# Two sums of a second attention moved into the last iterations of a graph attention, and a conditioning product cut into quarters

## The chip, the cores and the metric

The kernel runs on one core of a Trainium2 chip. The metric is the device time of one execution in microseconds, the median of the runs made of one kernel. One execution was also taken by the hardware profiler; all durations in this document come from such an execution.

## The reference

Two blocks follow each other on x of 4 batches x 1024 rows x 512 columns, all in float32.

- A graph attention. Each row goes through a linear layer (with a conditioning vector beside it), and then attends, with 16 heads and in two directions, to the first 20 rows of its batch; a mask of 11 labels gives each pair a bias and can switch it off. The result goes through relu and is added to x.
- A transformer block with adaptive normalization. The conditioning vector c (one row of 512 per batch) gives six rows of 512 by one product, the *modulation*:

```python
mod = silu(c) @ W_mod + b_mod                       # 512 -> 6 x 512
sh_msa, sc_msa, g_msa, sh_mlp, sc_mlp, g_mlp = split(mod, 6)
x = x + g_msa * attention(layernorm(x) * (1 + sc_msa) + sh_msa)   # 16 heads of 64, W_qkv, W_out, b_out
x = x + g_mlp * ff(layernorm(x) * (1 + sc_mlp) + sh_mlp)          # 512 -> 2048 -> 512, gelu
```

## The kernel before

Every instruction is issued in the order in which the program writes it: each engine (TensorE, VectorE, ScalarE, GpSimd, and SyncE, which starts the transfers) works off its own queue in that order, and waits between the engines come from the tiles that they share. A tile has a tag, and tiles of one tag take turns in as many buffers as the tag has; a new tile may be written only when the last reader of the tile before it in that buffer is done.

**Graph attention** (from about 60 to 418 us) is a loop `for s in range(-4, NTA + 2)` over 32 blocks of 128 rows. It is software-pipelined: iteration s works on several blocks at once, each in another step. In the order of one iteration, what matters here is:

- `g_load`, `g_loadmask`, `g_modload`: transfers that SyncE starts (block s + 4; weights of the modulation).
- `g_scores(s)` (TensorE, L710, 16 matmul passes into `pa`), then `g_weightsT(s - 1)` (TensorE, L759, five transposes of the finished weights `wts`, copied by ScalarE at L760).
- `g_soft1` to `g_soft5` (the softmax of block s): VectorE L723 (mask factor), GpSimd L733 (mask bias added), VectorE L740 and L741 (maximum, subtraction), ScalarE L744 (exp), VectorE L749 and L750 (sum, reciprocal), GpSimd L752 (`wts`). Between them `g_mask1(s + 3)` on GpSimd (L690, L692) and `g_mask2(s + 2)` on VectorE (L699 to L703).
- `g_self(s + 2)` (TensorE, L670), `g_selfT(s + 1)` (TensorE, L683, into a PSUM tile of tag `tr`, which has one buffer), `g_attend(s - 1)` (TensorE, L774).
- `g_rows(s - 1)` (VectorE, L786, and the store of the finished rows `x1d`, L787), `g_start(s + 3)` (VectorE, L658 and L659), `g_sum(s + 4)` (ScalarE, L646: the sum of each row of x, with the copy itself thrown into a tile `junk`).
- At the end of some iterations a round of the modulation, `g_mod(r)`. It multiplies half of the columns of several of the six rows: 16 matmuls of 256 columns into `pm` (tag `tr`, L811), four column groups of 32 beside each other. A round of kind 0 (shift and scale rows; r = 0 and 1, in iterations 6 and 12) is copied to `mrow` by ScalarE (L828), transposed by TensorE (L831, tag `tr`) and taken by VectorE into `modT` (L835, L839). A round of kind 1 (gate rows; r = 2 and 3, in iterations 22 and 29) is taken by VectorE straight from `pm` into `gates` (L820, L823). Their weights `wm` are loaded by `g_modload` in iterations 1, 7, 13 and 23.
- Rows of the second block's first batch that are already finished are normalized here: `norm_row` (VectorE, L389; iterations 15, 16, 22, 23) and `norm_T` (iterations 17 to 20 and 24 to 27): four transposes on TensorE into `ptn` (tag `tr`, L407), taken by ScalarE into `hT` (L412). The first query and key product (`ahead`, L442) follows in the last iterations.

**The second attention** uses a scheme of seven block products for every eight (`seven`, `with_two`), and so needs sums of blocks of the rows (`row_sums`: four subtractions of 128x1024, over `hT`, into `tx` and one in place) and of the weights (`weight_sums`: four of 128x256, into `ex` and one in place). For the first values of the first batch these sums stand between the two stages. VectorE forms the row sums (L579, L580, L584, L586) and GpSimd the weight sums (L468 to L471):

```python
first_sums, more_sums = row_sums(0)
first_sums()
for k in range(2):
    more_sums(k, nc.vector)
emit(-3, 0)                          # weight_sums on GpSimd, among others
for s in range(NS + 1):
    ...                              # scores, maximum, exp, scaling, transposes of step s
```

Each step s of that loop computes scores (TensorE, L1079, `psc`), their maximum (VectorE, L1090), exp (ScalarE, L1096), the division by the sum (ScalarE L1103, GpSimd L1105) and transposes (VectorE, L1114, with SyncE's transfers, L1118). A planner puts the products of the next queries, keys and values (TensorE, L497, with copies by ScalarE, L508, L519, and additions by VectorE, L511), the weighted values (L1041) and the output projections (L1059) between the scores.

Of the kernel before, what the change touches and what calls it, by code (L numbers as in the profile page):

```python
# [12 lines left out]
F32 = mybir.dt.float32  # L13
I32 = mybir.dt.int32
AF = mybir.ActivationFunctionType
ALU = mybir.AluOpType
# [3 lines left out]
P = 128  # L20
S = 1024
F = 512
# [19 lines left out]
def cond_block_kernel(  # L42
# [32 lines left out]
    def row(ap):  # L75

        return ap.unsqueeze(0)
# [54 lines left out]
    with ExitStack() as gctx:  # L132
# [9 lines left out]
        scT = gp.tile([P, FC, 32], F32, name="scT")  # L142
        wb = gp.tile([P, NL], F32, name="wb")
        bb = gp.tile([P, 1], F32, name="bb")
        bmB = gp.tile([P, F], F32, name="bmB")
        boB = gp.tile([P, F], F32, name="boB")


        lp = gctx.enter_context(tc.tile_pool(name="lp", bufs=1, reuse_waits="tile"))
# [219 lines left out]

        rp = ctx.enter_context(tc.tile_pool(name="rp", bufs=1, side="right", reuse_waits="tile"))  # L370
        qp = ctx.enter_context(tc.tile_pool(name="qp", bufs=1, side="right", reuse_waits="tile"))
        VB = 4
        xl, hT, wqk, wv, qT, kT, w1g, part = {}, {}, {}, {}, {}, {}, {}, {}
        NORM = ((x1d, mv1, rs1, nm1, SH_A, SC_A), (x2d, mv2, rs2, nm2, SH_M, SC_M))
# [189 lines left out]
        def of_weights(key, w, which, c):  # L564
# [3 lines left out]
            h, f = PIECE[which]  # L568
            return w[:, 2 * f + c, h, :]

        def row_sums(b):

            tx[b] = xp.tile([P, 6, F], F32, name="tx", tag="tx")
            h0, h1 = hT[0, 2 * b], hT[0, 2 * b + 1]
            o = [tx[b][:, 2 * k : 2 * k + 2, :] for k in range(3)]
            b11, b12, b21, b22 = h0[:, :2, :], h1[:, :2, :], h0[:, 2:, :], h1[:, 2:, :]

            def one():
                nc.vector.tensor_tensor(o[0], b12, b11, ALU.subtract)  # L579
                nc.vector.tensor_tensor(o[1], b22, o[0], ALU.subtract)  # L580

            def two(k, e=nc.gpsimd):
                if k == 0:
                    e.tensor_tensor(b12, b22, b12, ALU.subtract)  # L584
                else:
                    e.tensor_tensor(o[2], b21, o[1], ALU.subtract)  # L586

            return one, two
# [53 lines left out]
        def g_sum(i):  # L642

            nzs[i] = wp.tile([P, 1], F32, name="nz", tag="nz", bufs=4)
            junk = wp.tile([P, F], F32, name="junk", tag="junk", bufs=1)
            nc.scalar.activation(junk, xs[i], AF.Copy, accum_out=nzs[i])  # L646

        def opened(t):

# [139 lines left out]

        mods = {}  # L790

        CW = F // 2

        def g_modload(r):
            kind, half = divmod(r, 2)
            if r == 2:
                for k, (at, bias) in enumerate(((2 * F, b_out), (5 * F, b2))):
                    nc.sync.dma_start(bmB[64 * k : 64 * (k + 1)], row(b_mod[at : at + F]).broadcast_to([64, F]))
                    nc.sync.dma_start(boB[64 * k + 32 : 64 * k + 64], row(bias).broadcast_to([32, F]))
            mods[r] = wp.tile([P, FC, 4, CW], F32, name="wm", tag="wm", bufs=1)  # L800
            for k, blk in enumerate(((0, 1, 3, 4), (2, 5))[kind]):
                at = blk * F + half * CW
                nc.sync.dma_start(mods[r][:, :, k, :], w_mod[:, at : at + CW].rearrange("(c p) f -> p c f", p=P))

        def g_mod(r):

            kind, half = divmod(r, 2)
            pm = ps.tile([P, F], F32, name="pm", tag="tr")
            for c in range(FC):
                for k in range(4):  # L810
                    nc.tensor.matmul(  # L811
                        pm[32 * k : 32 * (k + 1), :CW],
                        lhsT=scT[:, c, :],
                        rhs=mods[r][:, c, k if kind == 0 else k // 2, :],
                        start=(c == 0),
                        stop=(c == FC - 1),
                    )
            cols = slice(half * CW, (half + 1) * CW)
            if kind == 1:
                nc.vector.tensor_tensor(gates[:, cols], pm[:, :CW], bmB[:, cols], ALU.add)  # L820
                for k in (1, 3):
                    q = slice(32 * k, 32 * (k + 1))
                    nc.vector.tensor_tensor(gates[q, cols], gates[q, cols], boB[q, cols], ALU.mult)  # L823
                if half == 1:
                    nc.sync.dma_start(gated, gates)
                return
            mrow = wp.tile([P, F], F32, name="mrow", tag="junk", bufs=1)
            nc.scalar.copy(mrow[:, :CW], pm[:, :CW])  # L828
            pt = ps.tile([P, 2, 4, 32], F32, name="ptm", tag="tr")
            for c in range(2):  # L830
                nc.tensor.transpose(pt[:, c].rearrange("p k b -> p (k b)"), mrow[:, c * P : (c + 1) * P], ident)  # L831
            for k, blk in enumerate((0, 1, 3, 4)):
                v = V_MOD + blk * FC + 2 * half
                o = modT[:, k * FC + 2 * half : k * FC + 2 * half + 2, :]
                nc.vector.tensor_tensor(  # L835
                    o, pt[:, :, k, :B], vecs[:, v : v + 2].unsqueeze(2).to_broadcast([P, 2, B]), ALU.add
                )
                if k % 2 == 1:
                    nc.vector.tensor_scalar(o, o, 1.0, None, ALU.add)  # L839

# [17 lines left out]
        for s in range(-4, NTA + 2):  # L858
            do(g_load, s + 4)
            if s >= -2:  # L860
                do(g_loadmask, s + 4)
            if s in (1, 7, 13, 23):
                g_modload(s // 6)
            do(g_scores, s)
            if s == NTA:
                ahead(4)
            do(g_weightsT, s - 1)
            do(g_soft1, s)
            do(g_startscores, s + 1)
            do(g_startattend, s - 1)  # L870
            do(g_soft2, s)
            do(g_mask2, s + 2)
            do(g_mask1, s + 3)
            do(g_soft3, s)
            do(g_self, s + 2)
            if s >= NTA - 2:
                ahead((2, 1, 1, 0)[s - NTA + 2])
            do(g_selfT, s + 1)
            do(g_soft4, s)
            if 0 <= s - 2 < NTA:  # L880
                statistics(xs.pop(s - 2), mv1[:, s - 2, :], wp)
            do(g_soft5, s)
            do(g_attend, s - 1)
            do(g_selfout, s + 2)
            do(g_rows, s - 1)
            do(g_start, s + 3)
            do(g_sum, s + 4)

            if s in (6, 12, 22, 29):
                g_mod((s - 5) // 6 - s // 29)  # L890
            if s == 12:
                rstd(rs1, mv1, nm1, 0, NT)
            if s in (14, 21):
                norm_load(0, s // 7 - 2)
            if 15 <= s - s // 22 * 7 <= 16:
                for i in range(2):
                    norm_row(0, s // 22 * VB + 2 * ((s - 15) % 7) + i)
            if s in (17, 18, 19, 20, 24, 25, 26, 27):
                norm_T(0, s // 24, (s - 17) % 7, bank_l0)
            if s == 25:  # L900
                load_qk(0, 0)
                load_v(0, 0)
                load_qk(0, 1)
# [3 lines left out]

    xp = ctx.enter_context(tc.tile_pool(name="xp", bufs=1, side="right", reuse_waits="tile"))  # L910
    vp = ctx.enter_context(tc.tile_pool(name="vp", bufs=1, side="right", reuse_waits="tile"))
    octx = ctx.enter_context(ExitStack())
    op_ = octx.enter_context(tc.tile_pool(name="op", bufs=1, side="right", reuse_waits="tile"))
# [2 lines left out]
    with ExitStack() as actx:  # L916
# [55 lines left out]

        def short():
            return op_.tile([P, F], F32, name="s", tag="s", bufs=1)

        def home_ex():
            return xp.tile([P, 3 * HB], F32, name="ex", tag="ex", bufs=1)

        def qk_sums(b, gp):
            weight_sums(nc.gpsimd, ("qk", b, gp), wqk[b, gp], home_ex)  # L980
# [182 lines left out]
        for b in range(B):  # L1163
            s0 = b * NP * NT
            for kind, n, lo, hi in ORDER:
                if b == 0 and lo < 8:
                    if (kind, n) == ("qk", 0):
                        ends[kind] = ends[kind][1:]
                        continue
                    lo, hi = (0, 0) if kind == "v" else (4, 4)  # L1170
                units, load, sums, steps = (
                    (1, load_qk, qk_sums, qk_steps) if kind == "qk" else (1.05, load_v, v_sums, v_steps)
                )
                if b > 0 or lo >= 8:
                    old = ends[kind].pop(0)
                    if old is not None:
                        behind.append((len(fill), old, 1))
                    add(-1, -1, 0, 0, load, b, n)
                if chain:
                    behind.append((len(fill), chain[-2], 0))  # L1180
                add(-1, -1, 0, 4, sums, b, n)
                add_steps(s0 + lo, s0 + hi, units, steps(b, n))
                ends[kind].append(chain[-1])
            for gp in range(NP):
# [166 lines left out]
                for _, k in sorted((f[3], k) for k, f in enumerate(fill) if where[k] == s):  # L1351
                    fill[k][4]()

        first_sums, more_sums = row_sums(0)
        first_sums()
        for k in range(2):
            more_sums(k, nc.vector)
        emit(-3, 0)
        before = None
        for s in range(NS + 1):  # L1360
# [224 lines left out]
```

## Time and profile before

| | |
|---|---|
| median of 3 runs | 3083.87 us (3083.62 to 3086.13) |
| the profiled execution | 3087.44 us, its span 3085.6 us |
| granted TensorE clock, mean | 0.998 |
| TensorE matmuls, busy | 3036.6 us, 98% of the span |
| VectorE, ScalarE, GpSimd, busy | 64%, 46%, 38% |
| TensorE's waits from 60 to 418 us, largest | 4.6 us for `wts` (L752), 2.2 us for `mrow` (L828) |
| TensorE's waits from 418 to 520 us, largest | 2.3 us for `w` (L1096), 1.9 us for `q` (L511) |

In a row of the timeline the first number is the start in microseconds from the start of the span, the second the duration from the first start to the last end of the merged instructions; then the engine (PE = TensorE, PEld = its weight loads, DVE = VectorE, ACT = ScalarE, POOL = GpSimd, SP = SyncE), the line of the kernel, the operation, output<-inputs, sizes, and how many instructions the row stands for. Square brackets give the idle time of the engine just before, and what ended it.

### The profile page before, as it was taken

What the parts mean: (1) busy time and instruction counts of PE and PEld (TensorE: products, weight loads), DVE (VectorE), ACT (ScalarE), POOL (GpSimd) and SP (SyncE); (2) the same over time, 40 slices, a digit from 0 to 9 for tenths busy, and PEclk for the clock granted to TensorE, in tenths of its full rate; (3) what the DMA queues carried; (4) which work ended last, traced back from release to release, by engine and by line L of the source; (5) the groups of instructions that cost most, each with busy time, mean ns of one, the idle gap of its engine ahead of it and who ended that gap; (6) DMA issues with size and microseconds to landing.
All of it is one profiled execution on the core that took longest, in us unless ns stands there. A gap on an engine that the chain in (4) does not pass through costs nothing.

```text
span 3085.6 us, 40768 instructions
## 1 busy us (share of the span) xinstructions
PE 3036.6 (98%) x14977; PEld 1918.0 (62%) x14977; DVE 1982.7 (64%) x2772; ACT 1420.5 (46%) x2351; POOL 1187.9 (38%) x729
## 2 busy tenths in 40 slices
PE   9999999999999999999999999999999999999999
PEld 5666655455455455455455455455568888888888
DVE  3788867777878777778777778777764332223222
ACT  2444456555655555655555655555641221112211
POOL 1444446455455554455545454654531101111010
PEclk9999999999999999999999999999999999999999
DMA  6433438677778766777776777776772011101110
GB/s 193 127 128 110 130 98 202 154 167 165 187 176 202 176 160 165 190 175 192 179 169 157 185 183 179 184 174 150 191 184 87 27 35 41 48 14 42 35 41 14
DMA packets 281882, 418.00 MB, mean 135 GB/s; under 512 B 28272, under 2 KB 100012, under 8 KB 281684
## 3 DMA queue, kind: packets, MB, share of 16 engines
q1 hardware_dynamic: 281436, 415.05, 53.1%
q8 instruction: 120, 1.97, 0.3%
q14 instruction: 78, 0.64, 0.1%
q10 hardware_dynamic: 248, 0.34, 0.0%
HBM read 121.09 MB, written 25.76 MB: 48 GB/s over the span
## 4 chain that ended last, share of the span: by engine, by line
PE 75%; DVE 7%; DMA 4%; ACT 4%; SPq 3%; issue 3%; POOL 3%; POOLq 0%; ACTq 0%; DVEq 0%
PE q L497 16%; PE psc L1079 13%; PE pav L1041 13%; PE pout L1059 7%; PE mbd L497 5%; PE mbu L497 5%; PE mad L497 3%; PE mau L497 3%; SPq L1118 2%; ACT w L1096 2%; PE mcd L497 2%; PE mdd L497 2%; DMA wT<-wd 2%; PE mdu L497 2%; PE mcu L497 2%
## 5 line engine op out<-in xcount | busy, mean ns | idle before, releaser
L1105 POOL TENSOR_SCALAR w<-w,sm 128x1024 f32<-128x1024 f32 x256 | 733.3, 2864 | 887.9 <-DVE sm L1101 876.2
L1096 ACT ACTIVATE w<-psc,mx 128x1024 f32<-128x1024 f32 x512 | 570.6, 1114 | 650.8 <-DVE mx L1090 649.7
L1114 DVE STREAM_TRANSPOSE wd<-w 128x1024 f32<-128x1024 f32 x512 | 633.6, 1238 | 132.7 <-ACT w L1103 115.9
L1090 DVE TENSOR_REDUCE mx<-psc 128x1 f32<-128x1024 f32 x512 | 599.4, 1211 | 100.8 <-PE psc L1079 97.9
L1079 PE MATMUL psc<-kT,qT 64*128 64x512 f32 x2048 | 530.0, 615 | 7.9 <-ACT w L1096 5.3
L1041 PE MATMUL pav<-wT,v 128*64 128x256 f32 x4096 | 476.4, 382 | 2.6 <-DMA wT<-wd 2.4
L1041 PEld LDWEIGHTS pav<-wT,v 128*64 128x64 f32 x4096 | 291.0, 137 | 226.0 <-issue 65.8
L1079 PEld LDWEIGHTS psc<-kT,qT 64*128 64x128 f32 x2048 | 203.3, 186 | 261.8 <-issue 154.9
L1103 ACT ACTIVATE w<-w,sm 128x1024 f32<-128x1024 f32 x256 | 291.0, 1137 | 0.0
L1059 PE MATMUL pout<-wout,oT 128*128 128x512 f32 x512 | 241.7, 605 | 0.0
L476 POOL TENSOR_TENSOR tx<-hT 128x512 f32<-128x512 f32 x8 | 10.2, 1269 | 601.4 <-DVE hT L414 601.4
L497 PE MATMUL q<-hT,wqk 128*128 128x512 f32 (+1 forms) x396 | 185.6, 593 | 7.3 <-DVE q L511 7.3
L1059 PEld LDWEIGHTS pout<-wout,oT 128*128 128x128 f32 x512 | 92.2, 189 | 129.3 <-issue 116.3
L710 PE MATMUL pa<-kp,sfT 128*128 128x320 f32 x512 | 143.5, 433 | 1.4 <-ACT sfT L685 1.4
L519 ACT COPY mbu<-mau 128x512 f32<-128x512 f32 x30 | 17.1, 570 | 276.4 <-PE mau L497 269.8
L1067 DVE TENSOR_TENSOR xr<-pout,xr 128x512 f32<-128x512 f32 x128 | 85.5, 680 | 90.1 <-PE pout L1059 90.0
L497 PEld LDWEIGHTS q<-hT,wqk 128*128 128x128 f32 x396 | 73.6, 191 | 103.8 <-issue 100.2
L497 PE MATMUL q<-tx,ex 128*128 128x512 f32 (+1 forms) x264 | 126.5, 603 | 0.0
L710 PEld LDWEIGHTS pa<-kp,sfT 128*128 128x128 f32 x512 | 94.8, 190 | 38.2 <-ACT sfT L685 1.9
L670 PE MATMUL pf<-wx,xT 128*128 128x512 f32 x256 | 116.3, 597 | 0.9 <-DVE pf L659 0.9
L497 PE MATMUL mad<-w,hs 128*128 128x256 f32 x512 | 113.1, 379 | 0.0
L497 PEld LDWEIGHTS mad<-w,hs 128*128 128x128 f32 x512 | 97.3, 190 | 13.2
(285 smaller groups left out, 4214.1 us busy)
## 6 DMA issues: line engine op xcount, KB each, us to landing
wT<-wd SPq DMA_DIRECT2D x1024, 256.0 KB
wqk<-in_w_qkv SPq DMA_DIRECT2D x64, 256.0 KB
xT<-in_xt SPq DMA_DIRECT2D x32, 256.0 KB
xs<-in_x SPq DMA_DIRECT2D x32, 256.0 KB
x1d<-xs SPq DMA_DIRECT2D x32, 256.0 KB
xl<-x1d SPq DMA_DIRECT2D x32, 256.0 KB
wv<-in_w_qkv SPq DMA_DIRECT2D x32, 256.0 KB
xr<-x1d SPq DMA_DIRECT2D x32, 256.0 KB
```

What stands on the lines that cost most here:

```text
L497: nc.tensor.matmul(t[:, q * width : (q + 1) * width], lhsT=lhs(which, q, k), rhs=rhs(which, q, k), start=(fresh and q == 0 and k == 0), st ...
L670: nc.tensor.matmul(pfs[i], lhsT=xT[i][:, c, :], rhs=wx[:, c, :], start=False, stop=(c == FC - 1), skip_group_check=True,)
L710: nc.tensor.matmul(pas[i][:, n, :HF], lhsT=sfT2[i][:, c, :], rhs=kp[:, b, c, n * HF : (n + 1) * HF], start=False, stop=(c == FC - 1), skip ...
L1041: nc.tensor.matmul(po[j * D : (j + 1) * D, :], lhsT=vt[b, g][:, m, p * P + j * D : p * P + (j + 1) * D], rhs=w[:, j, :, m, :], start=(m == 0),
L1059: nc.tensor.matmul(po, lhsT=oT[b, 2 * g + p][:, n * P : (n + 1) * P], rhs=wout[b, g][:, p, :], start=(p == 0), stop=(p == 1),)
L1067: nc.vector.tensor_tensor(t, po, t, ALU.add)
L1079: nc.tensor.matmul(sc[j][:, n * F : (n + 1) * F], lhsT=qT[b, gp][q, t * P : (t + 1) * P], rhs=kT[b, gp][q, n * F : (n + 1) * F], start=Tru ...
L1090: nc.vector.tensor_reduce(mx, sc, axis=AX.X, op=ALU.max, negate=True)
L1096: nc.scalar.activation(w, sc, AF.Exp, bias=mx, accum_out=sm)
L1103: nc.scalar.mul(w, w, sm)
L1105: nc.gpsimd.tensor_scalar(w, w, sm, None, ALU.mult)
L1114: nc.vector.transpose(wd[j][:, :, at, :], wn.pop((b, gp, t, j)).rearrange("p (m k) -> p m k", k=U))
```

## The change

- The row sums for the first values are formed in the graph attention's last iterations: two of them in iteration 28 and one in iteration 29, on GpSimd; the fourth, which overwrites a part of `hT` that TensorE still reads there, stays behind the loop, and is on GpSimd too. The weight sums are formed in iteration 30, on GpSimd as before. For this the pool that holds `tx` and `ex` is opened before the loop.
- To make room in SBUF, the modulation goes in eight rounds of a quarter of the columns (128) in place of four of a half: kind 0 in iterations 3, 6, 9, 12, kind 1 in iterations 15, 18, 21, 24, each with its weights loaded two iterations earlier and, for kind 1, the bias rows in quarters too. The sum of each row of x writes its copy over x itself, and the tile `junk` is gone.

```diff
-        bmB = gp.tile([P, F], F32, name="bmB")
-        boB = gp.tile([P, F], F32, name="boB")
+        bmB = gp.tile([P, F // 4], F32, name="bmB")
+        boB = gp.tile([P, F // 4], F32, name="boB")
...
+        xp = ctx.enter_context(tc.tile_pool(name="xp", bufs=1, side="right", reuse_waits="tile"))
...
-            def one():
-                nc.vector.tensor_tensor(o[0], b12, b11, ALU.subtract)
-                nc.vector.tensor_tensor(o[1], b22, o[0], ALU.subtract)
+            def one(e=nc.vector):
+                e.tensor_tensor(o[0], b12, b11, ALU.subtract)
+                e.tensor_tensor(o[1], b22, o[0], ALU.subtract)
...
-            junk = wp.tile([P, F], F32, name="junk", tag="junk", bufs=1)
-            nc.scalar.activation(junk, xs[i], AF.Copy, accum_out=nzs[i])
+            nc.scalar.activation(xs[i], xs[i], AF.Copy, accum_out=nzs[i])
...
-        CW = F // 2
+        CW = F // 4
...
-            kind, half = divmod(r, 2)
-            if r == 2:
+            kind, part_ = divmod(r, 4)
+            cols = slice(part_ * CW, (part_ + 1) * CW)
+            if kind == 1:
                 for k, (at, bias) in enumerate(((2 * F, b_out), (5 * F, b2))):
-                    nc.sync.dma_start(bmB[64 * k : 64 * (k + 1)], row(b_mod[at : at + F]).broadcast_to([64, F]))
-                    nc.sync.dma_start(boB[64 * k + 32 : 64 * k + 64], row(bias).broadcast_to([32, F]))
+                    at += part_ * CW
+                    nc.sync.dma_start(bmB[64 * k : 64 * (k + 1)], row(b_mod[at : at + CW]).broadcast_to([64, CW]))
+                    nc.sync.dma_start(
+                        boB[64 * k + 32 : 64 * k + 64], row(bias[cols]).broadcast_to([32, CW])
+                    )
...
-                nc.vector.tensor_tensor(gates[:, cols], pm[:, :CW], bmB[:, cols], ALU.add)
+                nc.vector.tensor_tensor(gates[:, cols], pm[:, :CW], bmB, ALU.add)
...
-            mrow = wp.tile([P, F], F32, name="mrow", tag="junk", bufs=1)
-            nc.scalar.copy(mrow[:, :CW], pm[:, :CW])
-            pt = ps.tile([P, 2, 4, 32], F32, name="ptm", tag="tr")
-            for c in range(2):
-                nc.tensor.transpose(pt[:, c].rearrange("p k b -> p (k b)"), mrow[:, c * P : (c + 1) * P], ident)
+            mrow = wp.tile([P, CW], F32, name="mrow", tag="mrow", bufs=1)
+            nc.scalar.copy(mrow, pm[:, :CW])
+            pt = ps.tile([P, 4, 32], F32, name="ptm", tag="tr")
+            nc.tensor.transpose(pt.rearrange("p k b -> p (k b)"), mrow, ident)
             for k, blk in enumerate((0, 1, 3, 4)):
-                v = V_MOD + blk * FC + 2 * half
-                o = modT[:, k * FC + 2 * half : k * FC + 2 * half + 2, :]
-                nc.vector.tensor_tensor(
-                    o, pt[:, :, k, :B], vecs[:, v : v + 2].unsqueeze(2).to_broadcast([P, 2, B]), ALU.add
-                )
+                v = V_MOD + blk * FC + part_
+                o = modT[:, k * FC + part_, :]
+                nc.vector.tensor_scalar(o, pt[:, k, :B], vecs[:, v : v + 1], None, ALU.add)
...
-            if s in (1, 7, 13, 23):
-                g_modload(s // 6)
+            if 1 <= s <= 22 and s % 3 == 1:
+                g_modload(s // 3)
...
-            if s in (6, 12, 22, 29):
-                g_mod((s - 5) // 6 - s // 29)
+            if 3 <= s <= 24 and s % 3 == 0:
+                g_mod(s // 3 - 1)
...
+            if s == 28:
+                first_sums, more_sums = row_sums(0)
+                first_sums(nc.gpsimd)
+            if s == 29:
+                more_sums(1)
+            if s == 30:
+                weight_sums(nc.gpsimd, ("v", 0, 0), wv[0, 0], home_ex)
...
-                add(-1, -1, 0, 4, sums, b, n)
+                if (kind, b, n) != ("v", 0, 0):
+                    add(-1, -1, 0, 4, sums, b, n)
...
-        first_sums, more_sums = row_sums(0)
-        first_sums()
-        for k in range(2):
-            more_sums(k, nc.vector)
+        more_sums(0)
         emit(-3, 0)
```

## The prediction

> **What bounds the kernel now.** I read the page's busy row first, then the list of what TensorE waits for, by stretch, and then the timeline of graph attention (60 to 418 us) and of the change to the second attention.
>
> ```profile
> PE 3036.6 (98%) x14977; PEld 1918.0 (62%) x14977; DVE 1982.7 (64%) x2772; ACT 1420.5 (46%) x2351; POOL 1187.9 (38%) x729
> ```
>
> TensorE has work for 98% of the span, so only its 49 us of idle time can be won, while anything put in its way is paid at once: it takes its instructions in order. Next the timeline of TensorE. Below, T(s) is the first L759 of graph attention's iteration s, and offsets such as +5.7 count from it.
>
> ```profile
> 127.99 0.75 PE L759 MATMUL pt<-ident,wts 128*128 128x128 f32 x5
> 137.93 0.76 PE L759 MATMUL pt<-ident,wts 128*128 128x128 f32 x5
> 143.66 1.93 PE L811 MATMUL pm<-wm,scT 128*32 128x256 f32 x32
> 146.68 0.44 PE L831 MATMUL ptm<-ident,mrow 128*128 128x128 f32 x2 [1.08 <-ACT mrow L828]
> 151.26 0.71 PE L759 MATMUL pt<-ident,wts 128*128 128x128 f32 x5
> 266.85 0.77 PE L759 MATMUL pt<-ident,wts 128*128 128x128 f32 x5 [0.30 <-POOL wts L752]
> 272.50 0.60 PE L407 MATMUL ptn<-ident,xl 128*128 128x128 f32 x4
> 277.25 0.71 PE L759 MATMUL pt<-ident,wts 128*128 128x128 f32 x5
> 307.65 0.74 PE L759 MATMUL pt<-ident,wts 128*128 128x128 f32 x5
> 313.37 1.93 PE L811 MATMUL pm<-wm,scT 128*32 128x256 f32 x32
> 319.64 0.71 PE L759 MATMUL pt<-ident,wts 128*128 128x128 f32 x5
> ```
>
> A plain iteration (127.99 to 137.93) lasts 9.94. One with a shift-and-scale round, s = 6, lasts 13.33: the round sits at +5.7 and TensorE stands until ScalarE has copied `mrow`. With a gate round, s = 22, it is 11.99; with norm_T's four transposes, s = 18, 10.40 (they stand at +5.65). Now VectorE:
>
> ```profile
> 275.94 1.36 DVE L659 SCALAR_TENSOR_TENSOR pf<-qrB,nz,bsB 128x512 f32<-128x512 f32 x1
> 318.00 0.41 DVE L820 TENSOR_TENSOR gates<-pm,bmB 128x256 f32<-128x256 f32 x1
> 339.78 1.36 DVE L659 SCALAR_TENSOR_TENSOR pf<-qrB,nz,bsB 128x512 f32<-128x512 f32 x1
> ```
>
> VectorE's queue ends an iteration with L659, and the gate round's L820 comes after that: at s = 22 TensorE ended `pm` at 315.2, and VectorE read it only at 318.00, +10.35. VectorE's own cycle is 9.95 (L723 to L723), just over TensorE's 9.85, so it has no room to come earlier. Last the place that is to become shorter, all engines:
>
> ```profile
> 418.82 1.22 DVE L579 TENSOR_TENSOR tx<-hT 128x1024 f32<-128x1024 f32 x1
> 420.19 2.02 PE L497 MATMUL q<-ex,tx 128*128 128x128 f32 x16 [0.22 <-DVE tx L579]
> 422.36 1.22 DVE L586 TENSOR_TENSOR tx<-hT,tx 128x1024 f32<-128x1024 f32 x1
> 423.49 2.35 DVE L1090 TENSOR_REDUCE mx<-psc 128x1 f32<-128x1024 f32 x2
> 426.00 3.11 PE L1079 MATMUL psc<-kT,qT 64*128 64x512 f32 x8 [2.00 <-ACT w L1096]
> 429.29 2.02 PE L497 MATMUL q<-ex,tx 128*128 128x128 f32 x16 [0.18 <-issue]
> ```
>
> Four row sums hold VectorE from 418.82 to 423.57, and the first maximum waits behind them although its scores were done at 420.0.
>
> **What the change takes away at that place.** The maximum then starts 2.0 after the scores (417.98), as at 476.41 to 478.43 where nothing is ahead of it: 420.0 for 423.49, 3.49 earlier. The second scores can start when the first value products end (423.8) and end at 425.8 for 429.1. The next products wait for ScalarE's copy L519 (ended 429.19), which moves with the maximum. So TensorE gains 3.3 to 3.5. I take 3.5. Its ends are 4.75 (all four sums) and 0 (see the rivals). The waits after that hang on VectorE and ScalarE, so they move along. `more_sums(0)` moves to GpSimd: a 128x1024 subtraction is about 2.4 there (256 columns take 0.72 and 512 take 1.27 to 1.28, so 2.1 ns each more); between TensorE's last read of hT at 416 and GpSimd's first own work (L1105, 427.37 now, 423.9 then) it has room; its reader is the third value step (435.9). The weight sums (4 x 0.72) ran on GpSimd at 411.2 to 414.1, under work: moving them wins nothing.
>
> **What the quarters cost: shift and scale, four rounds for two (s = 3, 6, 9, 12).** Now s = 6 takes 13.33 and s = 7 and 8 give back 0.13, since VectorE's cycle gets slack: 3.26 a round. The copy starts at +8.32 because ScalarE's queue holds exp, the `sf` copy and the sum of x before it, not because of `pm`: shorter matmuls win nothing. Won is 0.1 of the copy (0.37 for 256 columns) and one transpose of 0.13: 3.03 a round. Two more rounds, and two that are 0.23 shorter: 6.06 - 0.46 = 5.6. The six small VectorE operations a round (0.15 to 0.17) lie after L659, where such an iteration has over 2 us free.
>
> **Gates, four rounds for two (s = 15, 18, 21, 24 for 22, 29).** `pm` with 128 columns: no row shows it; half of 1.93 is 0.97, its 32 weight loads took 1.45; I take 1.0, and it matters only at s = 21. VectorE's three gate operations are 0.41 to 0.42 each at 256 columns; about 0.28 at 128 (640 columns take 0.82): 0.83.
> - s = 15: VectorE bounds s = 15 to 17 (norm_row's 0.99 twice), so its 0.83 is the cost.
> - s = 18: `pm` and norm_T's `ptn` share the one-buffer tag `tr`, and norm_T follows g_mod in TensorE's order. `ptn` may not be written before VectorE has read `pm`, and that stands behind L659, which ends at +10.45 (277.30 - 266.85). Read to +10.7; transposes 0.43, scores 4.31: 15.45 for 10.40, so 5.05. Everything queued on TensorE behind the transposes waits, the scores first.
> - s = 21: 11.05 for 9.84, 1.2. s = 22 loses its round: 9.85 for 11.99, -2.14. s = 23 no longer hides norm_row in that round: 10.89 for 10.13, +0.76.
> - s = 24: again `pm` before `ptn`, and here norm_row has pushed VectorE later: L659 ended at 341.14, +11.37. So 16.4 for 10.86, 5.5; s = 25 gets 0.1 back.
>
> Sum 0.83 + 5.05 + 1.2 - 2.14 + 0.76 + 5.5 - 0.1 = 11.1.
>
> **The last iterations.** GpSimd now:
>
> ```profile
> 380.08 1.27 POOL L752 TENSOR_TENSOR wts<-t,sm 128x640 f32<-128x640 f32 x1 [3.91 <-DVE sm L750]
> 382.71 1.54 POOL L733 TENSOR_TENSOR t<-t,add 128x640 f32<-128x640 f32 x1 [1.36 <-DVE t L723]
> 389.35 1.27 POOL L752 TENSOR_TENSOR wts<-t,sm 128x640 f32<-128x640 f32 x1 [5.11 <-DVE sm L750]
> ```
>
> Two sums of 2.4 go between the first two rows: from 381.35, or from 381.91 if they let VectorE's L659 end, to 386.2 or 386.7; L733 is then 3.5 to 4.0 later, and L740 to L752 behind it. L752 ends at 394.1 to 394.6 and T(30) is +12.7 to +13.3, for 11.98 with the gate round that goes from there: 0.7 to 1.3, 2.1 if a sum takes L1105's 2.85. I take 1.2. The one sum behind L752 at s = 29 and the weight sums at s = 30 delay L733 by 1.2 and 1.7; GpSimd's last row then ends 0.0 and 0.6 before TensorE needs it, so nothing.
>
> A rule on this: L659 takes 0.76 at 59.93, alone, and 1.36 wherever L752 runs, ending 0.55 after it. The Trainium skill, "SBUF — State Buffer", "SBUF: two separate sides", says that a VectorE operation with two SBUF inputs and a GpSimd operation that reads SBUF hold a port for a whole instruction, the other fully blocked. By the rule the later start holds (+13.3) and it speaks against sums on GpSimd beside VectorE; without it the term would be 0.7, and the total 0.5 less.
>
> **At nothing.** SyncE issues 40 transfers for 16; an iteration's regular ones take 2.0 us of it and four of `wm` 2.75, of 9.9, and behind them only x1d's store waits. A round's 1 MB has two iterations to land; without that cover its wait stands on TensorE at +5.7. Each bias load waits for VectorE's reading three iterations before. The sum of x written in place is the same instruction (0.63).
>
> **Sum.** 5.6 + 11.1 + 1.2 - 3.5 = +14.4. The profiled execution took 3087.44 (span 3085.6 and 1.84 around it), so 3101.8 for it; the median, 3083.87, is 3.57 lower, so 3098.3. A measurement of this kernel can tell about 0.2%, 6.2 us.
>
> **Rivals.** (A) The bank is free in time at s = 18 and 24: if VectorE reads `pm` by +6.7, the 5.05 + 5.5 go, and +3.9 is left, 3087.7, not slower by what can be told. For it: no row of now shows a `ptn` after a `pm`. Against: 318.00, +10.35. It decides where 8.2 of the two stalls' 10.55 are gone: there the sum falls under 6.2. (B) The 3.5 are given back: from 449 to 466 the chain of waits runs through SyncE's issues and the landing of `xr` (4.84), and a transfer that starts no earlier eats them: +17.9, 3101.8. Against: these issues wait for VectorE's transposes, which move too. (C) Faster: with A, and with all 7.5 us that TensorE waits between 418 and 520 won, 17.9 - 10.55 - 7.5 = -0.15; faster by 6.2 needs two free rounds besides.
>
> **How the numbers follow.** The forecast has 0.72, with 3095 to 3102 of its own (the first maximum's ends to 4.75 and 2, rounds of 2.5 to 3.3, a GpSimd sum of 2.4 to 2.85); B 0.13, A 0.12, C 0.03. The range reaches to A and past B: 3087 to 3104. Slower is the forecast, B and a little of A less the doubt on the stalls' size, 0.82; same 0.14; faster 0.04.
>
> **What would show it.** Right: at s = 18 and 24 the `ptn` transposes idle some 4 to 5 us on VectorE's `gates`, periods of 15.4 and 16.4; four waits on `mrow` of about 1; T(30) - T(29) over 12.5; the first L1090 2.0 after L1079. Wrong: `ptn` at +6.7, or the second maximum no earlier against the end of graph attention than now.

## The result, and the profile after

The changed kernel took 3102.58 us (median of 4 runs, 3101.14 to 3103.38), the kernel before 3085.0 (4 runs): a ratio of 1.0052, 95% interval 1.0040 to 1.0064, or 17.6 us more. The forecast was 14.4 more. The profiled execution took 3101.14, its span 3099.3, 13.7 above that of before.

First the list of what TensorE waited for in the whole span (in total, times, the longest, all us):

```profile
PE ptn L408 <- DVE gates L827: 8.7, 2, 4.8
PE pt L762 <- POOL wts L755: 7.7, 7, 3.0
PE ptm L837 <- ACT mrow L835: 6.8, 4, 1.7
```

The first line is new: it is the bank `tr` (the one buffer of that tag in PSUM, where TensorE puts its results) in iterations 18 and 24, with TensorE's transposes behind VectorE's reading of `pm`. The waits for `mrow` were two and 2.2 us in all, and are four of 1.7. The wait for `wts` was 4.6, and has its longest, 2.96, behind the row sums. Now TensorE's timeline of the two iterations, and one row of VectorE's:

```profile
279.33 1.08 PE L818 MATMUL pm<-wm,scT 128*32 128x128 f32 x32
284.29 0.66 PE L408 MATMUL ptn<-ident,xl 128*128 128x128 f32 x4 [3.88 <-DVE gates L827]
284.78 6.16 PE L713 MATMUL pa<-kp,sfT 128*128 128x320 f32 x16
290.78 0.71 PE L762 MATMUL pt<-ident,wts 128*128 128x128 f32 x5
354.67 1.12 PE L408 MATMUL ptn<-ident,xl 128*128 128x128 f32 x4 [4.79 <-DVE gates L827]
355.58 6.88 PE L713 MATMUL pa<-kp,sfT 128*128 128x320 f32 x16
```

```profile
283.95 0.28 DVE L827 TENSOR_TENSOR gates<-pm,bmB 128x128 f32<-128x128 f32 x1
```

VectorE reads `pm` at 283.95, +10.4 in its iteration, and the transposes start at 284.29. What the forecast lacks is in the rows of the scores: 6.16 and 6.88 instead of 4.47. The view by windows shows why (window, its length, TensorE's busy time, the granted clock, the share of the transfer engines, GB/s):

```profile
279.00:284.20 5.20, 1.41 (x36) 1.00 0.16 54
284.20:287.50 3.30, 3.21 (x11) 0.67 0.79 243
287.50:290.80 3.30, 3.30 (x12) 0.81 0.30 79
```

After the wait the granted clock (as a share of full speed) is 0.67 and 0.81 in the mean of these windows, and the scores run slowly. Narrower windows show that it falls to a half, behind both waits:

```profile
284.30:285.30 1.00, 1.00 (x6) 1.00 0.74 234
285.40:288.70 3.30, 3.30 (x8) 0.50 0.54 170
288.80:290.70 1.90, 1.90 (x8) 1.00 0.38 97
354.70:360.40 5.70, 5.70 (x14) 0.50 0.57 178
```

By the trace's record of the clock it is at a half for 3.41 us from 285.34 on, and for 6.83 us from 353.61 on. Below, this is called a fall. Last GpSimd's row sums, and the start of the second attention (TensorE and VectorE):

```profile
402.87 2.81 POOL L583 TENSOR_TENSOR tx<-hT 128x1024 f32<-128x1024 f32 x1
405.76 2.36 POOL L584 TENSOR_TENSOR tx<-hT,tx 128x1024 f32<-128x1024 f32 x1
408.07 1.54 POOL L736 TENSOR_TENSOR t<-t,add 128x640 f32<-128x640 f32 x1
```

```profile
440.66 1.99 PE L1086 MATMUL psc<-kT,qT 64*128 64x512 f32 x8 [0.93 <-DVE xs L789]
442.72 2.36 DVE L1097 TENSOR_REDUCE mx<-psc 128x1 f32<-128x1024 f32 x2 [1.26 <-PE psc L1086]
```

L736 starts 5.1 after T(29) = 402.99, where it stood at 1.3. The first maximum comes 2.06 after the scores, for 5.5. Term by term, T(s) being the first transposition of the weights (now L762):

| place | forecast | profile |
|---|---|---|
| before iteration 1 | 0 | +0.3 |
| shift and scale rounds, to iteration 14 | +5.6 | +5.5 |
| iterations 15 to 17 | +0.83 | +0.94 |
| iteration 18 (17.19 for 10.40) | +5.05 | +6.79 |
| iterations 21 to 23 | -0.18 | -0.24 |
| iterations 24, 25 (29.52 for 21.26) | +5.4 | +8.26 |
| iterations 28 to 31 | +1.2 | +1.1 |
| first maximum | -3.5 | -3.4 |
| from the first division by the sum (L1112) to the end | 0 | -5.5 |
| sum | +14.4 | +13.7 |

Two rows are off by much, the bank's (two rows, 4.6 too low together) and the last, and in this execution they cancel. The experiments go after both.

### The profile page after: what moved, and what is told of

It is laid out like the page before. It is cut to its first block, busy times and chain, and to the rows that moved or that the text cites. A ratio compares the mean times of both kernels' runs of the same rounds, so it can differ in the third digit from the quotient of the medians.

```text
span 3099.3 us, 41066 instructions
## 1 busy us (share of the span) xinstructions
PE 3037.0 (98%) x15105; PEld 1922.2 (62%) x15105; DVE 1982.1 (64%) x2786; ACT 1420.1 (46%) x2353; POOL 1198.6 (39%) x733
## 4 chain that ended last, share of the span: by engine, by line
PE 77%; DVE 8%; ACT 4%; issue 3%; DMA 3%; POOL 3%; SPq 2%; POOLq 0%; ACTq 0%; DVEq 0%
PE q L498 16%; PE psc L1086 14%; PE pav L1048 13%; PE pout L1066 7%; PE mbd L498 5%; PE mbu L498 5%; PE mad L498 3%; PE mau L498 3%; ACT w L1103 2%; PE mcd L498 2%; PE mdd L498 2%; SPq L1125 2%; PE mdu L498 2%; PE mcu L498 2%; DMA wT<-wd 1%
## 5 line engine op out<-in xcount | busy, mean ns | idle before, releaser
L1112 POOL TENSOR_SCALAR w<-w,sm 128x1024 f32<-128x1024 f32 x256 | 733.8, 2867 | 875.7 <-DVE sm L1108 864.2
```

Of the source, the lines that this page charges most:

```text
L1112: nc.gpsimd.tensor_scalar(w, w, sm, None, ALU.mult)
```

## The experiments

The theory: the bank's two waits, and a clock that falls in them, are most of the loss; the eight rounds cost another 5.5; moving the sums wins 3.4 at the first maximum. The last row of the table has nothing to do with the change. The rivals: quarters cost by their number and small transfers, wherever they stand; the scores are slow because transfers land in the same microseconds; the sums on GpSimd are the loss.

**The kernel before, profiled again** (one execution, 3080.78).

> The kernel before, unchanged, for a second profile of it. In the changed kernel's profile the second attention and the rest ran 2658.6 us from its first scores to the end, in the profile of before 2667.6; the row sums explain 3.4 of these 9.0. If the other 5.5 are a matter of when transfers land and when TensorE's clock falls (two value products at 1246.8 and 1714.5 took 5.4 for 3.6 us in the profile of before, and not after), this stretch differs by some us here from 2667.6, and such products sit elsewhere or are missing. If the change itself won the 5.5, it is 2667.6 again within 1 us, with both slow products.

From the first scores to the end it ran 2660.8 (3079.0 less 418.16), 6.8 less than in the first profile of the same code. Here the row of each at the same place, the first profile, then this one:

```profile
1246.76 3.17 PE L497 MATMUL q<-hT,wqk 128*128 128x512 f32 x4 [2.34 <-DVE q L511]
```

```profile
1246.61 1.96 PE L497 MATMUL q<-hT,wqk 128*128 128x512 f32 x4 [1.86 <-DVE q L511]
```

In the first the wait was 2.34 and the granted clock behind it 0.64 (mean of 1246.7 to 1249); in the second it was 1.86 and the products ran at full speed. The mean clock was 0.998 there and 1.000 here. So the last row of the table needs no effect of the change, as two profiles of the same code differ by more: the changed kernel needs 2658.6 for this stretch in its profile, with one fall, and 2660.8 - 3.4 = 2657.4 would be expected without falls.

**The gate rounds in other iterations.**

```diff
+        LOAD_AT, MOD_AT = (1, 4, 7, 10, 13, 15, 19, 22), (3, 6, 9, 12, 14, 16, 21, 23)
-            if 1 <= s <= 22 and s % 3 == 1:
-                g_modload(s // 3)
+            if s in LOAD_AT:
+                g_modload(LOAD_AT.index(s))
-            if 3 <= s <= 24 and s % 3 == 0:
-                g_mod(s // 3 - 1)
+            if s in MOD_AT:
+                g_mod(MOD_AT.index(s))
```

> The changed kernel with the four gate rounds in iterations 14, 16, 21 and 23 instead of 15, 18, 21 and 24, none of them in an iteration with norm_T. If the two stalls of TensorE on the bank shared by pm and ptn (with the clock that falls in them) are what the change costs, 6.8 and 8.4 us go, some 1.5 come back where VectorE takes two more gate rounds beside norm_row: about 3089, and T(19)-T(18) and T(25)-T(24) are 10.3 to 10.9. If eight rounds as such, with their small transfers, are the cost and not where two of them stand, it stays within 3 us of 3102.6.

Measured: 3090.42 (11 runs), ratio to the kernel before 1.0018 (1.0009 to 1.0026), for 3084.35 there. Iterations 18 and 24 last 10.39 and 11.51 (10.3 to 10.9 were expected), and the wait of `ptn` is gone from the list. Eight rounds and the same transfers are still there, so the first rival falls. Iteration 30 lasts 11.60 here, for 9.90 in the changed kernel's profile:

```profile
402.45 0.77 PE L762 MATMUL pt<-ident,wts 128*128 128x128 f32 x5 [2.79 <-POOL wts L755]
403.05 5.29 PE L443 MATMUL pqk<-hT,wqk 128*128 128x512 f32 x8
```

Eight passes took 5.29, for 3.60 there: the clock fell (0.61 from 404 to 408) after the wait behind the row sums, too.

**The two waits filled with matmuls.**

```diff
                 g_mod(s // 3 - 1)
+                if s in (18, 24):
+                    t = ps.tile([P, KC0, P], F32, name="pfill", tag="wt")
+                    for _ in range(4 if s == 18 else 5):
+                        nc.tensor.matmul(
+                            t[:, :4, :].rearrange("p k q -> p (k q)"), lhsT=ident, rhs=wx[:, 0, :], start=True, stop=True
+                        )
```

> The changed kernel with four (iteration 18) and five (iteration 24) matmuls of 512 columns added between pm and ptn, whose result nobody reads: they keep TensorE busy while it waits for VectorE and end before that wait does. If the scores after the stalls took 6.2 and 6.9 instead of 4.5 us because the clock fell while TensorE stood idle, they take 4.5 again: T(19)-T(18) is 15.4 for 17.2, T(25)-T(24) 16.4 for 19.2, and the time falls by 4.6 to about 3098. If the scores were slow for another reason (the weight transfers that land in the same microseconds, 79% of the transfer engines busy), nothing changes, or the time rises.

```profile
279.97 3.70 PE L898 MATMUL pfill<-wx,ident 128*128 128x512 f32 x8
283.91 0.66 PE L408 MATMUL ptn<-ident,xl 128*128 128x128 f32 x4 [0.24 <-DVE gates L827]
284.41 4.47 PE L713 MATMUL pa<-kp,sfT 128*128 128x320 f32 x16
```

The transposes still begin when VectorE has read `pm`, but the scores take 4.47 again: iterations 18 and 24 last 15.50 and 16.40, the forecast's 15.45 and 16.4. The transfer engines were nearly as busy (0.70 from 284.2 to 287.5 for 0.79, with a clock of 1.00), so the second rival falls. The time did not follow: 3106.64 (5 runs, 3099.03 to 3109.42), ratio 1.0062 (1.0050 to 1.0075). It ran once more, beside the changed kernel itself:

> The changed kernel with the two waits filled with matmuls, once more: its first profile had iterations 18 and 24 at 15.5 and 16.4 us, 4.5 less, but four slow stretches in the rest, and a median of 3106.6 from five times between 3099.0 and 3109.4. If those slow stretches are chance, the median comes out some 4 us below that of the changed kernel on the same chip. If filling the waits in graph attention brings on falls later, it is again at or above it, and the profile again shows four or more slow stretches after 400 us.

> The changed kernel, unchanged, beside the next two on one chip. Graph attention's iterations repeat to 0.1 us, with 17.2 and 19.2 in iterations 18 and 24. If what differs between executions is only how often the clock falls at waits of 2 to 3 us later on (1.7 to 1.8 us each, none to five of them in the profiles so far), the times spread over 3098 to 3108 and the stretch from the first scores on is 2657 us plus 1.8 for each fall in it.

3100.38 with the fill (ratio 1.0050, 1.0037 to 1.0062), 3103.25 without it (1.0061, 1.0049 to 1.0073), the kernel before 3085.1. All ten times of the one have the median 3102.9, those of the other 3103.2: a gain in the whole time isn't shown. In the graph attention it is: 15.50 and 16.41 again, for 15.51 and 18.56 in this second profile of the changed kernel. There, iteration 18 kept its clock after the same wait of 3.88, while later a fall followed a wait of only 1.95 (the four passes of the last row took 3.45, for 1.88 at full speed):

```profile
284.68 0.66 PE L408 MATMUL ptn<-ident,xl 128*128 128x128 f32 x4 [3.88 <-DVE gates L827]
285.18 4.47 PE L713 MATMUL pa<-kp,sfT 128*128 128x320 f32 x16
1729.63 3.45 PE L498 MATMUL q<-hT,wqk 128*128 128x512 f32 x4 [1.95 <-DVE q L512]
```

The profiles with the fill show four and three falls after 400 us, those without it one and two (the drop behind TensorE's last product, which every profile has, left out). From the first scores to the end they took 2667.6 and 2666.1, for 2658.6 and 2660.6 without the fill. At 1.7 a fall, the falls explain only a part of this. Whether the fill costs there what it wins here, and by what way, stays open.

**The quarters alone.** The sums are back where they were.

```diff
-            if s == 28:
-                first_sums, more_sums = row_sums(0)
-                first_sums(nc.gpsimd)
-            if s == 29:
-                more_sums(1)
-            if s == 30:
-                weight_sums(nc.gpsimd, ("v", 0, 0), wv[0, 0], home_ex)
...
-        more_sums(0)
+        first_sums, more_sums = row_sums(0)
+        first_sums()
+        for k in range(2):
+            more_sums(k, nc.vector)
```

> The changed kernel with the row sums back on VectorE behind the loop, and the weight sums back there too: the quarters alone. If moving the sums wins 3.4 at the first maximum and costs 1.1 in iterations 28 and 29, this is 2.3 slower than the changed kernel, about 3104.9, with T(30)-T(29) back at 9.9 and 5.5 us from the first scores to the first maximum. If the sums on GpSimd cost more than they win (they delay the mask bias by 4 us), it is faster than the changed kernel.

Measured: 3103.96 (5 runs, 3099.34 to 3109.26), ratio 1.0062 (1.0048 to 1.0076): no different from the changed kernel. T(30) - T(29) is 9.93, and the first maximum starts again 5.4 after the scores (442.14 less 436.79). The expectation had subtracted wrongly: the 1.1 is what the sums cost against an iteration that held a gate round (11.98). Against the iteration as it is without one they cost 13.05 - 9.93 = 3.1, which eats the 3.4 they win. The third rival is half right: moved as they were, the sums win 0.3, if the clock holds. It doesn't always: the sums make TensorE wait 2.8 to 3.0 for `wts` at the start of iteration 30, and in three of the five profiles that have them there (the moved gate rounds and both with the fill) the clock fell behind that wait, and iteration 30 took 11.4 to 11.6 for 9.9. With the sums back on VectorE it fell behind another wait, that of the second scores for ScalarE, which took 4.31, for 3.11 in the kernel before (the granted clock was 0.50 from 445 to 448):

```profile
444.65 4.31 PE L1079 MATMUL psc<-kT,qT 64*128 64x512 f32 x8 [2.00 <-ACT w L1096]
```

So these runs don't show whether the move as a whole wins or loses.

**A rebuilt version.** The sums in six pieces of 128x512, one an iteration from 26 to 31; the gate rows in halves in iterations 16 and 22; a shift-and-scale quarter transposed one iteration after its product.

```diff
-            mods[r] = wp.tile([P, FC, 4, CW], F32, name="wm", tag="wm", bufs=1)
+            mods[r] = wp.tile([P, FC, 4 // (kind + 1), CW], F32, name="wm", tag="wm", bufs=1)
...
+            mrows[r] = mrow
+
+        def g_modT(r):
+
+            part_, mrow = r, mrows.pop(r)
...
+        LOAD_AT, MOD_AT = (1, 4, 7, 10, 13, 19), (3, 6, 9, 12, 16, 22)
...
+            if s in (4, 7, 10, 13):
+                g_modT(s // 3 - 1)
...
+            if s == 26:
+                pieces, more_sums = row_pieces(0)
+            if 26 <= s <= 31:
+                pieces.pop(0)()
```

> The sums stay in graph attention's last iterations, but in six pieces of 128x512, one in each of the iterations 26 to 31 (the weight sums and the in-place sum behind the loop). The gate rows go in two halves again, in iterations 16 and 22, away from norm_T. A shift-and-scale quarter is transposed one iteration after its matmuls, so that TensorE doesn't wait for ScalarE's copy. If the terms are right, against the kernel before: four rounds at 1.2 instead of two at 3.3 (-1.7), a gate round in iteration 16 (1.3) instead of 29 (2.1), pieces 1.0, first maximum -3.4: together -4.9, about 3080, and 9 to 14 us of the 18 to 23 that the changed kernel loses in graph attention are seen to come from the bank and the copy. If VectorE's cycle (9.95) takes the place of TensorE's waits, the rounds cost 3 again and the time is that of before or more.

Measured: 3081.57 (11 runs), ratio 0.9989 (0.9981 to 0.9998); beside the next one again 3083.12, ratio 0.9989 (0.9980 to 0.9998), the kernel before 3085.1 and 3086.53.

> The rebuilt version once more, beside the next one: iterations repeat to 0.1 us, the time about 3081.6.

The waits on `mrow` and on the bank are gone. The pieces cost nothing: iterations 28 to 30 last 9.84, 9.92 and 9.85 (1.0 was expected). But a round cost 2.0 to 2.4, not 1.2: VectorE took TensorE's place as the bound.

**VectorE's part in one operation.**

```diff
-            for k, blk in enumerate((0, 1, 3, 4)):
-                v = V_MOD + blk * FC + part_
-                o = modT[:, k * FC + part_, :]
-                nc.vector.tensor_scalar(o, pt[:, k, :B], vecs[:, v : v + 1], None, ALU.add)
-                if k % 2 == 1:
-                    nc.vector.tensor_scalar(o, o, 1.0, None, ALU.add)
+            v = vecs[:, V_MOD : V_MOD + 6 * FC].rearrange("p (g h c) -> p g h c", g=2, h=3)[:, :, :2, part_]
+            o = modT.rearrange("p (g h c) b -> p g h c b", g=2, h=2)[:, :, :, part_, :]
+            nc.vector.tensor_tensor(
+                o,
+                pt.rearrange("p (g h) b -> p g h b", g=2)[:, :, :, :B],
+                v.unsqueeze(3).to_broadcast([P, 2, 2, B]),
+                ALU.add,
+            )
...
+            if s == 0:
+                for blk in (1, 4):
+                    t = vecs[:, V_MOD + blk * FC : V_MOD + (blk + 1) * FC]
+                    nc.vector.tensor_scalar(t, t, 1.0, None, ALU.add)
```

> The rebuilt version with VectorE's six small operations behind each shift-and-scale round (0.17 each) made one, the added 1.0 put into the bias columns once before. In the rebuilt version such a round cost 2.4 us (11.13 + 10.17 + 10.87 for 29.81) where 1.2 were expected. If VectorE's cycle is what bounds these iterations, five operations fewer take 0.8 from each of the four rounds, in the iteration behind the transposes (10.87 to 10.73 become 9.9 to 10.1), and the time falls by 3 to about 3078.5. If TensorE's own work or its wait for the weights bounds them, they stay at 10.7 to 10.9 and the time at 3081.6.

```profile
129.61 0.16 DVE L858 TENSOR_TENSOR modT<-ptm,vecs 128x16 f32<-128x16 f32 x1
129.69 0.81 DVE L739 TENSOR_TENSOR t<-pa,mul 128x640 f32<-128x640 f32 x1
```

VectorE's next mask factor (L739) follows at once where five operations stood between. The iterations fell from 10.87 to 10.03, 10.73 to 9.89 (twice) and 10.87 to 10.02: 0.84 each, so VectorE was their bound. Measured: 3076.97 (12 runs), ratio to the kernel before 0.9971 (0.9960 to 0.9982): 9.6 us faster than it in the medians, and faster than both kernels of this study. The first scores start at 415.60, for 419.62 in the rebuilt version. Against that version, beside it, the median fell by 6.15, twice the 3 that were expected: 3.4 of it are these four iterations, 4.0 in all lie before the first scores, and the other 2.1 aren't explained.

## Why the prediction was right, and where it was off

- **The bank** was the right mechanism in the right two iterations, as its row L820 at +10.35 had told; rival A falls with the row of `ptn`, and moving the rounds took 11.5 us back (17.6 above the kernel before, then 6.1). Mis-sized was the price: "transposes 0.43, scores 4.31" put the scores at full clock after the wait. They took 6.0 and 6.7 to the next row; with the waits filled, the forecast's 15.45 and 16.4 came out within 0.05. The term, 10.55, measured 15.2.
- **The clock** is what that price lacked. The Trainium skill, "TensorE: Matmul & The Clock Gate", Part 1, states a rule on it: TensorE's clock halves after an idle window of about 3.4 us and comes back after a busy one, and the windows run freely. The traces agree on the windows. A fall lasts 3.41 us or twice that, and costs 1.7, half of it, when TensorE has work throughout. Within a profile the falls begin whole numbers of 3.413 us apart (285.34 and 353.61 in the changed kernel's are 20.0 of them apart). The traces don't agree that a window must be idle: the shortest wait with a fall behind it was 1.95. When the ten profiles with falls are divided into such windows, from 60 us on, all 25 falls follow a window in which TensorE ran no matmul for 1.95 us or more, and no window at full speed without a fall behind it has over 1.99. That also tells why the same wait of 3.88 had a fall in two profiles and none in a third: one window held 2.36 and 2.88 us of it there, while in the second profile of the changed kernel two windows shared it, 1.89 and 1.99.
- **Rounds.** 5.6 forecast, 5.5 measured, by the reason given: ScalarE's copy hardly starts sooner for a shorter `pm` (+8.17 in iteration 3, for +8.32). A wait on `mrow` is 1.7 instead of "about 1", since `pm` ends sooner while the copy stays.
- **Sums.** T(30) - T(29) is 13.05, inside 12.7 to 13.3. By the prediction's rule on the shared port the first sum starts when VectorE's L659 ends. Here L659's counterpart (L662) ends 0.59 after the sum's start, and the sum takes 2.81 instead of 2.36, which fits such a wait; the pieces of the rebuilt version take 1.72 in iterations 26 to 28, where they meet that operation, and 1.27 in 29 to 31, where it no longer runs. The net 1.2 was right, but it hid that the step itself costs 3.1, because the gate round that left iteration 29 was counted in it. The price of a fall behind the wait that the sums bring, 1.5 to 1.7, was not in it either.
- **The first maximum.** 3.5 forecast, 3.44 measured, and not given back (rival B falls): from the first scores on 2658.6 with one fall of the clock in it, for 2660.8 before with none. Rival B's 3101.8 is nearer to the measured 3102.6 than the forecast's 3098.3 all the same, by accident.
- **Not in the sum** was the spread of whole executions: each profile shows none to four falls of the clock, behind waits of 1.95 to 4.8 us, mostly at some 1.7 each. They are part of why the profiled execution shows 13.7 and the medians 17.6 and 18.2: the profile of before had three falls after 418, that of the changed kernel one. Without falls after 418 the working above would give 22.7 - 3.4 = 19.3. That 13.7 came so near to 14.4 is luck.
- **At nothing** were the transfers and the sum of x in place, rightly: iterations with neither a round nor a sum last as before (9.84 and 9.85 in iteration 2, 10.28 twice in 19).

## What to carry to other kernels

Before a step is put into an iteration of a software pipeline, list the tiles of its PSUM bank's tag in that iteration's order, and ask in which place of the reader's queue the reading stands: here two users met in a one-buffer bank, and a product of 1.1 us cost 6.8 and 8.4. An idle time of TensorE of 2 us or more is dearer than it looks, as the clock can fall behind it; a wait of 1.7 never had that price in these runs, those of 4.8 always did. When a change both takes work out of an iteration and puts other work in, cost the two apart: the sum of both hid that the move won no more than 0.3.

## What the runs showed of the hardware

- The clock falls after some waits: after 1.7 (four rounds in each of six profiles) and 1.86 never, after 1.95 to 2.96 in some profiles, after 3.59 in the one that has it, after 3.88 in two of three, after 4.79 in all three. It depends on where the wait lies against windows of 3.41 us: some 2 us of idle time within one were enough. Behind it the granted clock was 0.50, for 3.41 or 6.83 us; the 0.61 to 0.81 above are means of windows that hold full speed too.
- Matmuls of 32 weight columns in four column groups: 16 (32 in the rows, which count two passes each) of 128 columns took 1.08, of 256 columns 1.93.
